# A fused transformer block in float32: where the tiles begin in a partition of the on-chip memory

## The chip, the cores and the metric

The kernel runs on one core of one Trainium2 chip. A core has five engines that run side by side: TensorE (PE in the profile; its weight loads have a row of their own, PEld), VectorE (DVE), ScalarE (ACT), GpSimd (POOL) and SyncE (SP), which here only issues DMAs. Operands lie in SBUF, an on-chip memory of 128 partitions; a tile is a range of bytes that is the same in every partition. Matmul results land in PSUM. The metric is the device time of one execution in microseconds; the span of a profile runs from the first instruction to the last.

## The reference

16 sequences of 256 tokens with 256 channels go through one block: self-attention with 16 heads of 16 channels, cross-attention to 256 context tokens, and an MLP of 1024 hidden channels.

```python
c_proj = silu(c) @ W_mod + b_mod            # six rows of 256 per sequence
x_norm = ln(x) * (1 + scale_a) + shift_a
q, k, v = split(x_norm @ W_qkv + b_qkv)
x = x + gate_a * (softmax(q k^T * scale) v @ W_proj + b_proj)
q_c = ln(x) @ W_qc + b_qc
k_c, v_c = split(ln(context) @ W_kvc + b_kvc)
x = x + softmax(q_c k_c^T * scale) v_c @ W_cproj + b_cproj
h = gelu((ln(x) * (1 + scale_m) + shift_m) @ W_mlp1 + b_mlp1)
x = x + gate_m * (h @ W_mlp2 + b_mlp2)
```

## The kernel before

**Stages.** A short start loads and splits weights. Then 32 units follow, one for each attention of each sequence (16 of self-attention, kind `s`, and 16 of cross-attention, kind `c`); work for units ahead and behind is woven into each unit. The last stage, from about 555 us, is the MLP of 16 sequences in four chunks of 256 hidden channels each.

**Precision.** A float32 factor is kept as two tiles of the matmul type float32r, a high part and the remainder: `xTh` and `xTl` for activations, `wqch` and `wqcl` and their like for weights. A product is three matmuls, high by high, high by low and low by high. Every such matmul has 256 columns of moving operand (1024 bytes of a partition) and 128 columns of weights (512 bytes), and each loads its own weights first. In the call `PE.matmul(out, weights, moving)` the second argument is the loaded one.

**The matmuls by their name in the profile** (a name is output tile, arrow, operands; the profile lists the operands by the alphabet, not by their role):

- `s` and `st` from `big`, during the units: scores and transposed scores (`s_tile`, `t_part`). Weights and moving operand are both slices of one tile `big`, which holds the stacked q and k of a unit.
- `ps_q`, `ps_k`, `ps_qc`, `ps_kc`, `ps_h`: projections with the weight matrix loaded and the activations moving (`lane`, with `tok` false). `ps_v_s`, `ps_v_c`, `ps_P_s`, `ps_P_c`: projections with the activations loaded and the matrix moving (`tok` true). Each is a lane of 12 matmuls on partitions 0 to 63 and 12 on partitions 64 to 127; `beside` issues two lanes at a time, one on each half of the partitions, so that two matmuls of 64 rows run side by side.
- `o` from `pt`, `v`: probabilities times values, four matmuls of 32 weight columns side by side (`av_part`), in plain float32.
- `psT`, `psA`, `psm`: transposes, with the identity tile `ident` moving and the data loaded.
- `ph` (`mlp_first`): first MLP product on all 128 rows; weights are slices of `wself` (which holds W_mlp1 by then), and the moving operand is `wkch`/`wkcl` or `wqch`/`wqcl`, which hold the transposed activations by then. Twelve per chunk.
- `st` or `s` from `big`, `hh`/`hl` (`mlp_second`): second MLP product on all 128 rows; weights are slices of `hh`/`hl`, and the moving operand is `big[2]`, which holds W_mlp2. Twelve per chunk.

**Order.** The lists `E_` and `PLAN` and the class `InOrder` fix the order of instructions on each engine. Line 51 is that class, through which every operation goes, so that all rows of the profile name it; groups are told apart by their tiles.

**Where tiles lie.** A pool takes a range of each partition. Pools stand behind one another in the order in which the code opens them, and within a pool tiles with their buffers stand in the order of their first use, each padded to a multiple of 32 bytes. Before the change there are two such pools, `const` and `work`, and small tiles stand between large ones.

Of the kernel before, what the change touches and what calls it, by code (L numbers as in the profile page):

```python
# [10 lines left out]
F32 = mybir.dt.float32  # L11
F32R = mybir.dt.float32r
# [4 lines left out]
P = 128  # L17
# [4 lines left out]
def pixart_block(  # L22
# [8 lines left out]
    B, N, H = x.shape  # L31
# [3 lines left out]
    NT = N // P  # L35
    KC = H // P
# [22 lines left out]

    const = ctx.enter_context(tc.tile_pool(name="const", bufs=1))  # L60
    work = ctx.enter_context(tc.tile_pool(name="work", bufs=2))
    dram = ctx.enter_context(tc.tile_pool(name="dram", bufs=2, space=bass.MemoryType.DRAM))
    psum = ctx.enter_context(tc.tile_pool(name="psum", bufs=2, space=bass.MemoryType.PSUM))

# [10 lines left out]
        return psum.tile([P, 512], F32, tag=tag, name=name, bufs=2)  # L75


    wz = const.tile([P, P], F32, name="wz")
    DVE.memset(wz, 0.0)
    ident = const.tile([P, P], F32, name="ident")  # L80
    make_identity(nc, ident)
    mhalf = const.tile([P, 2], F32, name="mhalf")
    POOL.memset(mhalf, -0.5)

    big = [const.tile([P, 2, 8, N], F32R, name=f"big{i}") for i in range(3)]
    vts = [const.tile([P, NT, NH, 32], F32, name=f"v{i}") for i in range(3)]
    mxs = [const.tile([P, 160], F32, name=f"mx{i}") for i in range(3)]
    for t_ in mxs:
        POOL.memset(t_, 0.0)
    wself = const.tile([P, 16, H], F32R, name="wself")  # L90
# [11 lines left out]
    def tok(ap, b):  # L102
        return ap[b].rearrange("(t p) h -> p t h", p=P)
# [5 lines left out]
    brow = const.tile([32, P], F32, name="brow")  # L109

    def by_parity(w):
        return w.rearrange("p k (c f) -> p k f c", f=2)

# [11 lines left out]
    def wtile(name, c):  # L125
        return [const.tile([P, KC, c], F32R, name=f"{name}{s}") for s in ("h", "l")]
# [41 lines left out]
    dummy = const.tile([P, 2], F32, name="dummy")  # L168

    def f_load():  # L170
        X[0] = work.tile([P, NT, H], F32, tag="x", name="x_0", bufs=5)
# [152 lines left out]
    def layernorm(src, name):  # L324

        o = Box()

        def stats():
            o.st = work.tile([P, NT, 6], F32, tag="bnst", name=f"st_{name}")
            for t in range(NT):  # L330
                DVE.bn_stats(o.st[:, t], src()[:, t])

        def rstd(power=True):
            o.mv = work.tile([P, NT, 2], F32, tag="bnmv", name=f"mv_{name}")
            for t in range(NT):
                DVE.bn_aggr(o.mv[:, t], o.st[:, t])
            o.rs = work.tile([P, NT], F32, tag="rstd", name=f"rs_{name}")
            if power:
                o.pow()

        def pow():
            POOL.tensor_scalar(o.rs, o.mv[:, :, 1], EPS, None, ALU.add)
            POOL.tensor_tensor(o.rs, o.rs, mhalf, ALU.pow)

        def apply(eng=E_['LN'].get(name[0])):
            o.xn = work.tile([P, NT, H], F32, tag="xn", name=f"xn_{name}", bufs=3)
            for t in range(NT):
                if eng == "act":
                    ACT.activation(o.xn[:, t], src()[:, t], AF.Identity, bias=o.nb[:, t:t + 1],
                                   scale=o.rs[:, t:t + 1])  # L350
                else:
                    (DVE if eng == "dve" else POOL).tensor_scalar(
                        o.xn[:, t], src()[:, t], o.mv[:, t, 0:1], o.rs[:, t:t + 1],
                        ALU.subtract, ALU.mult)

        def shift():
            o.nb = work.tile([P, NT], F32, tag="nb", name=f"nb_{name}")
# [249 lines left out]
    def bc_t(ap):  # L607
        return ap.unsqueeze(1).to_broadcast([P, NT, H])
# [25 lines left out]
    def build_post(u):  # L634

        b, name = u.b, f"{u.kind}{u.b}"
        W = Wp if u.kind == "s" else Wcp
        o = Box()

        def begin():  # L640
            if u.kind == "c":
                return
            G[b] = work.tile([P, 2, H], F32, tag="g", name=f"g_{b}", bufs=3)
            SP.dma_start(G[b].rearrange("p a h -> p (a h)"),
                         gd[b, 0:2].rearrange("a h -> (a h)").partition_broadcast(P))

        def gate():
            if u.kind == "c":
                return
            o.xg = work.tile([P, NT, H], F32, tag="x1", name=f"xg_{b}", bufs=7)  # L650
            POOL.tensor_tensor(o.xg, X[b], bc_t(G[b][:, 1]), ALU.add)

        def pieces(hf):
            o.ps = ps_gen(f"psA{hf}_{name}", SHORT)
            return [u.oT[hf][:, r, t * P:(t + 1) * P] for t in range(NT) for r in range(2)]

        def turn(hf):
            whole(pieces(hf), o)

        def halves(hf):  # L660
            return half_turns(pieces(hf), o)

        def norm(hf):
            if hf == 0:
                o.A = work.tile([P, NT, H], F32, tag="A", name=f"A_{name}", bufs=1)
            pv = o.ps.rearrange("p (x h c) -> p x h c", x=4, h=4)
            rc = work.tile([P, 4, 4, 1], F32, tag="rc", name=f"rc{hf}_{name}")
            DVE.reciprocal(rc, pv[:, :, :, HD:HD + 1])
            A = o.A.rearrange("p t (r f) -> p (t r) f", r=2)[:, :, 64 * hf:64 * hf + 64]
            DVE.tensor_tensor(A.rearrange("p x (h i) -> p x h i", h=4),  # L670
                              pv[:, :, :, 0:HD], rc.to_broadcast([P, 4, 4, HD]), ALU.mult)

        aT = transposed(lambda: o.A, f"a{name}", pool=True)

        def proj(half):

            if half == 0:
                o.ps = ps_gen(f"psP_{name}")
            for t in range(NT):
                for k in range(KC):  # L680
                    for a, b in (((1, 0),) if half else ((0, 0), (0, 1))):
                        PE.matmul(o.ps[:, t * H:(t + 1) * H], aT.xT[a][:, k, t * P:(t + 1) * P], W[b][:, k],
                                  start=(half == t == k == b == 0), stop=(half == 1 and t == NT - 1 and k == KC - 1),
                                  skip_group_check=True)

        def end():
            t1 = work.tile([P, NT, H], F32, tag="t1", name=f"t1_{name}")
            o.t1 = t1
            ACT.copy(t1.rearrange("p t h -> p (t h)"), o.ps)

        def add():
            t1 = o.t1
            if u.kind == "s":
                POOL.tensor_tensor(t1, t1, bc_t(G[b][:, 0]), ALU.mult)
                X1[b] = o.xg
                POOL.tensor_tensor(X1[b], o.xg, t1, ALU.add)
            else:
                POOL.tensor_tensor(t1, t1, X1[b], ALU.add)
                o.out = t1

        def store():
            if u.kind == "c":
                SP.dma_start(tok(X2d, b), o.out)

        def finish():
# [119 lines left out]
    for n, (kind, b) in enumerate(seq):  # L825
        u = Box()
# [209 lines left out]
    for n, v in (("0", u0), ("1", u1), ("2", u2)):  # L1036
        for c in "KQV":
            o = getattr(v, c)
# [58 lines left out]
    for i in range(3):  # L1097
        b = i if i < 2 else 0
        u = ahead_of_mlp(nu + i, b)
# [158 lines left out]
    last, o, q = units[-1], units[-1].post, units[-2].post  # L1258
# [97 lines left out]
```

## Time and profile before

| | us |
|---|---|
| three runs | 738.65, 738.64, 736.59 (median 738.64) |
| span of the profiled execution | 737.1 |
| PE busy | 728.8 |
| PEld busy | 643.6 |
| DVE busy | 583.4 |
| ACT busy | 556.2 |
| POOL busy | 546.9 |

The span is the profiled execution's own time as far as the profile shows it; it lies within the three runs, 1.5 below their median and 0.5 above the lowest. In the profile's rows "x128" is a count, "271/277/281" is the least, the median and the greatest duration in ns, and the ends of matmuls are modelled, so the rate at which they follow one another is read from their starts. A duration of 277 ns with a start every 115 ns means that matmuls overlap in the array's pipeline.

### The profile page before, as it was taken

How to read it: one execution, taken by the hardware profiler on the slowest of the kernel's cores; microseconds unless marked ns; L12 is line 12 of the kernel's file. 1: busy time of each engine (PE TensorE's matmuls, PEld its weight loads, DVE VectorE, ACT ScalarE, POOL GpSimd, SP SyncE). 2: the span in 40 equal slices, each digit the busy share in tenths (PEclk: the TensorE clock that was granted, in tenths of full speed). 3: DMA queues.
4: the chain of work that ended last, by engine and by line, in shares of the span. 5: the costliest groups of instructions: out<-in, count | busy, mean ns of one | idle time of the engine just before them, and what ended most of it. 6: DMA issues, size and time to landing. Idle time of an engine off the chain costs nothing.

```text
span 737.1 us, 24900 instructions
## 1 busy us (share of the span) xinstructions
PE 728.8 (99%) x10104; PEld 643.6 (87%) x10104; DVE 583.4 (79%) x1218; ACT 556.2 (75%) x961; POOL 546.9 (74%) x574
## 2 busy tenths in 40 slices
PE   9999999999999999999999999999999999999997
PEld 8888888888888888888888888888888999999997
DVE  3788898989888898988888888888745676786872
ACT  3357888888888888888888888899886665566663
POOL 6687769769696876969687898878746767767743
PEclk8899999999999999999999999999999999999999
DMA  5554243333425334342533444344211423333222
GB/s 162 203 179 145 104 174 118 122 140 119 145 96 182 117 129 148 119 145 100 178 117 138 147 156 150 118 151 148 95 60 44 116 58 101 87 100 102 83 61 57
DMA packets 67109, 90.56 MB, mean 123 GB/s; under 512 B 6194, under 2 KB 38740, under 8 KB 66996
## 3 DMA queue, kind: packets, MB, share of 16 engines
q1 hardware_dynamic: 66164, 86.88, 35.4%
q8 instruction: 80, 1.31, 0.7%
q0 software_dynamic: 560, 1.84, 0.7%
q14 instruction: 33, 0.27, 0.1%
q10 hardware_dynamic: 272, 0.26, 0.1%
HBM read 26.97 MB, written 8.46 MB: 48 GB/s over the span
## 4 chain that ended last, share of the span: by engine, by line
PE 95%; DVE 2%; POOL 1%; ACT 1%; issue 1%; POOLq 0%; ACTq 0%; DVEq 0%
PE s L51 18%; PE o L51 16%; PE st L51 16%; PE ph L51 11%; PE ps_qc L51 5%; PE ps_q L51 5%; PE ps_kc L51 4%; PE ps_k L51 3%; PE ps_v_c L51 3%; PE ps_P_s L51 3%; PE ps_v_s L51 3%; PE ps_P_c L51 2%; PE ps_h L51 1%; PE psT_q L51 1%; PE psA_c L51 1%; PE psA_s L51 1%
## 5 line engine op out<-in xcount | busy, mean ns | idle before, releaser
L51 DVE TENSOR_REDUCE mx<-s 128x2 f32<-128x512 f32 x504 | 324.5, 684 | 62.8 <-PE s L51 56.8
L51 ACT ACTIVATE pt<-st 128x1024 f32<-128x1024 f32 x252 | 259.1, 1028 | 16.6 <-PE st L51 11.0
L51 PE MATMUL s<-big 63*128 63x256 f32 (+1 forms) x1024 | 185.0, 298 | 0.5 <-DVE mx L51 0.2
L51 PEld LDWEIGHTS s<-big 63*128 63x128 f32 (+1 forms) x1024 | 132.9, 185 | 19.6 <-DVE l_kc L51 6.6
L51 PE MATMUL st<-big 64*128 64x256 f32 (+1 forms) x1024 | 134.0, 297 | 0.1
L51 POOL TENSOR_TENSOR hl<-hf,hh 128x512 fp32r<-128x512 f32 x64 | 85.5, 1340 | 54.0 <-ACT hh L51 53.6
L51 PE MATMUL o<-pt,v 128*32 128x256 f32 x2048 | 123.8, 382 | 0.0
L51 PEld LDWEIGHTS st<-big 64*128 64x128 f32 (+1 forms) x1024 | 96.2, 185 | 14.9 <-issue 12.8
L51 PEld LDWEIGHTS o<-pt,v 128*32 128x32 f32 x2048 | 60.0, 109 | 41.5
L51 ACT ACTIVATE hf<-ph,bT 128x256 f32<-128x256 f32 x114 | 47.9, 472 | 33.6 <-PE ph L51 33.6
L51 ACT ACTIVATE hh<-ph,bT 128x256 fp32r<-128x256 f32 x114 | 48.0, 473 | 25.1 <-PE s L51 13.1
L51 ACT COPY oT<-o 128x512 f32<-128x512 f32 x63 | 37.0, 587 | 32.8 <-PE o L51 32.8
L51 PE MATMUL st<-big,hh 128*128 128x256 f32 x256 | 45.3, 277 | 0.0
L51 PE MATMUL s<-big,hh 128*128 128x256 f32 x256 | 45.2, 277 | 0.0
L51 PE MATMUL ps_k<-xTh_s,wself 64*128 64x256 f32 (+1 forms) x232 | 44.8, 298 | 0.1
L51 PE MATMUL ph<-wkch,wself 128*128 128x256 f32 x224 | 44.7, 283 | 0.0
L51 PE MATMUL ph<-wqch,wself 128*128 128x256 f32 x224 | 44.6, 283 | 0.0
L51 PE MATMUL ps_q<-xTh_s,wself 64*128 64x256 f32 (+1 forms) x240 | 41.1, 287 | 0.0
L51 POOL TENSOR_SCALAR xn_c<-c,mv_c,rs_c 128x256 f32<-128x256 f32 x32 | 39.1, 1230 | 1.7
L51 PE MATMUL ps_v_s<-wself,xTh_s 64*128 64x256 f32 x224 | 38.8, 293 | 0.0
L51 PEld LDWEIGHTS st<-big,hh 128*128 128x128 f32 x256 | 38.8, 188 | 0.0
L51 PEld LDWEIGHTS s<-big,hh 128*128 128x128 f32 x256 | 38.8, 188 | 0.0
(256 smaller groups left out, 2505.2 us busy)
## 6 DMA issues: line engine op xcount, KB each, us to landing
big<-h_kc SPq DMA_DIRECT2D x32, 256.0 KB
big<-h_qc SPq DMA_DIRECT2D x32, 256.0 KB
big<-h_k SPq DMA_DIRECT2D x30, 256.0 KB
big<-h_q SPq DMA_DIRECT2D x29, 256.0 KB
g<-gd SPq DMA_DIRECT2D x16, 256.0 KB
c<-in_ctx_dram SPq DMA_DIRECT2D x16, 256.0 KB
big<-l_kc SPq DMA_DIRECT2D x16, 256.0 KB
big<-l_qc SPq DMA_DIRECT2D x16, 256.0 KB
```

What stands on the lines that cost most here:

```text
L51: i = f(*a, **k)
```

## The change

Two pools are added and two tiles are moved to the front of `const`: `brow` (512 bytes) and `bqkv` (384 bytes) now fill the space up to byte 17408, which is 17 times 1024. Then every tile in `const` and `work` has a size that is a multiple of 1024 bytes. Small constants go to the pool `edge`, and statistics and other small work tiles go to `tiny`; both lie behind `work`. No instruction is added, removed or moved on any engine, the waits and the numbers of buffers are the same, and the sizes are the same. Only start addresses differ. The table has the start of the first buffer of each tile in its partition, and what is left of it beyond a multiple of 256; the other buffers of a tile leave the same remainder unless three are given.

| tile | before | left over 256 | after | left over 256 |
|---|---|---|---|---|
| `big` | 17568 | 160 | 17408 | 0 |
| `v` | 66720 | 160 | 66560 | 0 |
| `wself` | 80928 | 32 | 78848 | 0 |
| `wqch`, `wqcl`, `wkch` to `wcpl` | 98848 | 32 | 96256 | 0 |
| `qkh` (`h_q`, `h_k`, `hh`) | 119008 | 224 | 114688 | 0 |
| `pt` | 125152 | 224 | 120832 | 0 |
| `x` | 145632 | 224 | 141312 | 0 |
| `xn`, `A`, `g`, `x1`, `xTh`, `xTl`, `qkl` (`l_q`, `l_k`, `hl`), `y` | 156128 | 224 | 151552 | 0 |
| `c`, `oT` | 216032 | 224 | 210944 | 0 |
| `t1` | 224352 | 96 | 219136 | 0 |
| `ident` | 17024 | 128 | 223744 | 0 |
| `mx` (three) | 79008 | 160, 32, 160 | 224288 | 32, 160, 32 |
| `m` | 215520 | 224 | 227808 | 224 |

Slices of these tiles that a float32r matmul reads begin at multiples of 512 bytes from the tile's start, so that they leave the tile's own remainder. Of `v` the slices begin at multiples of 128.

```diff
+    edge = ctx.enter_context(tc.tile_pool(name="edge", bufs=1))
+    tiny = ctx.enter_context(tc.tile_pool(name="tiny", bufs=2))
...
-    wz = const.tile([P, P], F32, name="wz")
+    brow = const.tile([32, P], F32, name="brow")
+    bqkv = const.tile([P, 6, B], F32, name="bqkv")
+    wz = edge.tile([P, P], F32, name="wz")
...
-    ident = const.tile([P, P], F32, name="ident")
+    ident = edge.tile([P, P], F32, name="ident")
...
-    mxs = [const.tile([P, 160], F32, name=f"mx{i}") for i in range(3)]
+    mxs = [edge.tile([P, 160], F32, name=f"mx{i}") for i in range(3)]
...
-    cpT = const.tile([P, 12, B], F32, name="cpT")
-    bqkv = const.tile([P, 6, B], F32, name="bqkv")
-    sc1 = const.tile([P, 2, 2, B], F32, name="sc1")
-    bT = const.tile([P, 40], F32, name="bT")
-    sT = const.tile([P, KC, B], F32, name="sT")
+    cpT = edge.tile([P, 12, B], F32, name="cpT")
+    sc1 = edge.tile([P, 2, 2, B], F32, name="sc1")
+    bT = edge.tile([P, 40], F32, name="bT")
+    sT = edge.tile([P, KC, B], F32, name="sT")
...
-            o.st = work.tile([P, NT, 6], F32, tag="bnst", name=f"st_{name}")
+            o.st = tiny.tile([P, NT, 6], F32, tag="bnst", name=f"st_{name}")
...
-            rc = work.tile([P, 4, 4, 1], F32, tag="rc", name=f"rc{hf}_{name}")
+            rc = tiny.tile([P, 4, 4, 1], F32, tag="rc", name=f"rc{hf}_{name}")
...
-        m = work.tile([P, P], F32R, tag="m", name=f"m_{u.n}_{hf}", bufs=1)
+        m = tiny.tile([P, P], F32R, tag="m", name=f"m_{u.n}_{hf}", bufs=1)
```

`mhalf`, `dummy`, `mv`, `rs` and `nb` move in the same way.

More of the change, by code (lines that the diff above doesn't have):

```diff
@@ L75, in ps_gen @@
         return psum.tile([P, 512], F32, tag=tag, name=name, bufs=2)
-    wz = const.tile([P, P], F32, name="wz")
+    brow = const.tile([32, P], F32, name="brow")
+    bqkv = const.tile([P, 6, B], F32, name="bqkv")
+    wz = edge.tile([P, P], F32, name="wz")
     DVE.memset(wz, 0.0)
-    ident = const.tile([P, P], F32, name="ident")
+    ident = edge.tile([P, P], F32, name="ident")
     make_identity(nc, ident)
-    mhalf = const.tile([P, 2], F32, name="mhalf")
+    mhalf = edge.tile([P, 2], F32, name="mhalf")
     POOL.memset(mhalf, -0.5)
@@ L107, in load_x @@
         SP.dma_start(X[b], tok(x, b))
-    brow = const.tile([32, P], F32, name="brow")
     def by_parity(w):
@@ L167, in pixart_block @@
     wm0, wm1, wk, wq, wv = (ts[i // 2][:, i % 2] for i in range(5))
-    dummy = const.tile([P, 2], F32, name="dummy")
+    dummy = edge.tile([P, 2], F32, name="dummy")
     def f_load():
@@ L333, in rstd @@
         def rstd(power=True):
-            o.mv = work.tile([P, NT, 2], F32, tag="bnmv", name=f"mv_{name}")
+            o.mv = tiny.tile([P, NT, 2], F32, tag="bnmv", name=f"mv_{name}")
             for t in range(NT):
                 DVE.bn_aggr(o.mv[:, t], o.st[:, t])
-            o.rs = work.tile([P, NT], F32, tag="rstd", name=f"rs_{name}")
+            o.rs = tiny.tile([P, NT], F32, tag="rstd", name=f"rs_{name}")
             if power:
@@ L356, in shift @@
         def shift():
-            o.nb = work.tile([P, NT], F32, tag="nb", name=f"nb_{name}")
+            o.nb = tiny.tile([P, NT], F32, tag="nb", name=f"nb_{name}")
             POOL.tensor_scalar(o.nb, o.mv[:, :, 0], -1.0, None, ALU.mult)
```

## The prediction

> **What bounds the kernel now.** I read the page's head and its chain first, then the busy time by stage, then PE's rows in the stages.
>
> ```profile
> span 737.1 us, 24900 instructions
> PE 728.8 (99%) x10104; PEld 643.6 (87%) x10104; DVE 583.4 (79%) x1218; ACT 556.2 (75%) x961; POOL 546.9 (74%) x574
> PE 95%; DVE 2%; POOL 1%; ACT 1%; issue 1%; POOLq 0%; ACTq 0%; DVEq 0%
> ...
> 0.00:40.00 40.00, 38.12 (x242) 33.36 (x243) 22.34 (x57) 13.05 (x31) 25.73 (x38) 0.87 0.55 182
> 40.00:555.00 515.00, 514.49 (x8359) 435.25 (x8361) 438.46 (x936) 435.81 (x677) 402.35 (x432) 1.00 0.38 133
> 555.00:590.00 35.00, 33.57 (x292) 32.77 (x285) 21.89 (x41) 22.47 (x52) 25.16 (x23) 1.00 0.30 84
> 590.00:733.00 143.00, 142.59 (x1222) 142.17 (x1221) 99.75 (x184) 84.84 (x203) 93.61 (x83) 1.00 0.30 82
> ```
>
> PE carries 95% of the chain. By stage (the first number after the comma is PE's busy time, the third from the end the granted clock) it idles 0.5 us of the 515 us of units and 0.4 us of the 143 us of MLP, both at full clock. No other engine is near its limit. So a faster DMA or a shorter wait has at most the idle time of the start and of 555 to 590 us to win, and what the change can do to the time is done through the rate at which matmuls follow each other. That rate is not one number. In the MLP both products have the same shape and the array never pauses:
>
> ```profile
> 649.33 0.39 PE L51 MATMUL st<-big,hh 128*128 128x256 f32 x2
> 649.55 0.28 PE L51 MATMUL st<-big,hl 128*128 128x256 f32 x1
> 649.67 0.39 PE L51 MATMUL st<-big,hh 128*128 128x256 f32 x2
> 649.89 0.28 PE L51 MATMUL st<-big,hl 128*128 128x256 f32 x1
> 650.01 0.39 PE L51 MATMUL st<-big,hh 128*128 128x256 f32 x2
> ...
> 650.58 0.40 PE L51 MATMUL ph<-wqch,wself 128*128 128x256 f32 x2
> 650.82 0.28 PE L51 MATMUL ph<-wqcl,wself 128*128 128x256 f32 x1
> 650.94 0.40 PE L51 MATMUL ph<-wqch,wself 128*128 128x256 f32 x2
> 651.18 0.28 PE L51 MATMUL ph<-wqcl,wself 128*128 128x256 f32 x1
> 651.30 0.40 PE L51 MATMUL ph<-wqch,wself 128*128 128x256 f32 x2
> ```
>
> Six matmuls of the second product take 650.01 - 649.33 = 0.68 us, 113.3 ns each. Six of the first take 651.30 - 650.58 = 0.72 us, 120.0 ns each. It is not chance, since every matmul of a kind agrees (least/median/greatest ns):
>
> ```profile
> L51 PE MATMUL st<-big,hh x196: 276/276/279, 589.8 to 725.7; 128*128 128x256 f32 x196
> L51 PE MATMUL ph<-wqcl,wself x100: 282/283/283, 590.6 to 727.1; 128*128 128x256 f32 x100
> ```
>
> What differs is where the operands lie. While one matmul streams its moving operand, the weights of the next are loaded, so I take the distance from the next weights' start to the moving operand's start, beyond a multiple of 256. For `ph` it is 32 - 32 = 0; for the second product 160 - 224, that is 192. The units show the same with 64 rows, two lanes side by side:
>
> ```profile
> 301.47 0.28 PE L51 MATMUL ps_qc<-xTh_q,wqch 64*128 64x256 f32 x1
> 301.48 0.28 PE L51 MATMUL ps_P_c<-wcph,xTh_ac 64*128 64x256 f32 x1
> ...
> 302.51 0.27 PE L51 MATMUL ps_qc<-xTl_q,wqch 64*128 64x256 f32 x1
> 302.55 0.28 PE L51 MATMUL ps_P_c<-wcph,xTl_ac 64*128 64x256 f32 x1
> ...
> 302.83 0.24 PE s L51 x4
> 303.07 0.24 PE st L51 x4
> ```
>
> Each lane has ten starts here, nine steps. `ps_qc` (moving 224, weights 32, distance 192) takes 1.04 / 9 = 115.6 ns a step; `ps_P_c` at the same moment, with the roles exchanged (distance 64), takes 1.07 / 9 = 118.9. The last two rows are from the chain: four score matmuls, two on each half, in 0.24 us, 120 ns a step, with both operands in `big`, distance 0. Distance 0 gives 120 in both places, 192 gives 113 to 116. I read this as two streams that hinder each other when they begin at the same place of a 256-byte round.
>
> **The change, part by part.** After it every float32r operand leaves 0, so every distance is 0, the slowest value seen.
>
> *Second MLP product, on the path.* Its distance goes from 192 to 0, its step from 113.3 to 120.0.
>
> ```profile
> L51 PE MATMUL st<-big,hh 128*128 128x256 f32 x256 | 45.3, 277 | 0.0
> L51 PE MATMUL s<-big,hh 128*128 128x256 f32 x256 | 45.2, 277 | 0.0
> L51 PE MATMUL st<-big,hl 128*128 128x256 f32 x128 | 35.4, 277 | 0.0
> L51 PE MATMUL s<-big,hl 128*128 128x256 f32 x128 | 35.4, 277 | 0.0
> ```
>
> 768 matmuls by 6.7 ns are 5.1 us. PE is the only bound there, so all of it reaches the end. ACT and POOL then wait a little longer for each chunk, which costs nothing. `ph` keeps its distance: 0.
>
> *Lanes, on the path.* Lanes that load the matrix (1584 matmuls in 40 to 555 us, 792 on each half) go from distance 192 to 0, those that load the activations (1440, 720 on each half) from 64 to 0. First and last of the grouped rows:
>
> ```profile
> L51 PE MATMUL ps_qc<-xTh_q,wqch x128: 272/277/364, 108.2 to 514.4; 64*128 64x256 f32 x128
> L51 PE MATMUL ps_P_c<-wcph,xTl_ac x112: 272/276/361, 168.9 to 544.0; 64*128 64x256 f32 x112
> ```
>
> If each lost what the steps above leave to 120, that is 792 x 4.4 + 720 x 1.1 = 4.3 us. Where a quick lane runs beside a slow one the slow one ends the piece, and only 1.1 ns is lost: 1512 x 1.1 = 1.7 us. Both pairings occur; I take 3.0.
>
> *Scores*: 2016 matmuls within `big`, distance 0 before and after: 0.
>
> *Attention values and transposes.*
>
> ```profile
> L51 PE MATMUL o<-pt,v x2044: 379/379/404, 49.6 to 555.0; 128*32 128x256 f32 x186
> L51 PE MATMUL psA_s<-ident,oT 64*128 64x64 f32 x256 | 29.3, 227 | 0.0
> ```
>
> `o` has distances of 64 and 192 by turns (slices of `v` lie 128 bytes apart) and yet least equals median, so I take 0. Its bound is 512 groups of four by 6.7 ns, 3.4 us either way. The 1296 transposes go from distance 160 to 0; two halves side by side at 3.3 ns a step bound that at 2.1 us either way, and I take 0, as a 64-column stream has little time to collide.
>
> *DMAs.* Rows of 1024 and 2048 bytes now begin at multiples of 1024. The cover is PE's own work, idle 0.5 us in the units; without that cover the gain could reach the 1.9 us that PE idles in the first 40 us, where loads are waited for. I take 0. [...]
>
> *Elementwise work* on DVE, ACT and POOL keeps its shapes, and none of these engines is the bound: 0.
>
> Sum: 5.1 + 3.0 = 8.1 us on a span of 737.1, 745.2. The span stands 1.5 below the median of the runs, which gives 746.7.
>
> **The rivals.**
>
> *Faster: the start itself counts, not the distance.* Then 32 beyond a multiple of 256 is a bad start (`ph`, 120.0), 224 a good one, and 0 may be the best. The MLP alone cannot separate this from the distance, since a cost for the moving start and one for the weights' start would fit both of its rows. If all went at the best rate seen, 113.3, `ph` would win 672 x 6.7 = 4.5 us, the lanes 792 x 2.3 + 720 x 5.6 = 5.9, the scores 1008 steps x 6.7 = 6.8: 17.2 in all, 721.5. Against it: the same tile `big`, moving, goes at 120 beside weights at 160 and at 113.3 beside weights at 224, and exchanging the roles in the lanes exchanges the rates. Where it decides: if all five groups take one common step r, the time is unchanged at r = (768 x 113.3 + 672 x 120 + 1008 x 120 + 792 x 115.6 + 720 x 118.9) / 3960 = 117.6 ns; below that the change gains.
>
> *No change: addresses are indifferent.* The two rates would come from something else that goes with the kind of matmul, say the PSUM tile or who reads it, and the time stays at 738.6. Against it: `ps_qc` and `ps_P_c` have one shape and one kind of output and differ at the same moment. [...]
>
> **How the numbers follow.** A measurement of this kernel can tell about 0.3% from no change, 2.2 us. Forecast with its mechanism 0.62: its own range goes from the lanes' and the MLP's loss half as large (742.7) to all bounds together, 5.1 + 4.3 + 3.4 + 2.1 = 14.9 (753.5). Faster rival 0.25, from 736 down to 721.5, most of it where a part of the matmuls gains. No change 0.13. A range of 728 to 753 leaves out about a third of the faster rival and a tenth of the forecast, under 2 in 10 together. Slower 0.62, same 0.13, faster 0.25.
>
> **What would show it.** Right: six matmuls of the second product in 0.72 us, their median at 283 ns as `ph`, `ph` itself unchanged, `ps_qc` at 118 ns a step or more, scores unchanged. Wrong on the mechanism: `ph` off 120 though its distance is kept. Wrong on the size: lanes that restart after each wait and never settle, so that they keep their rate. If PE's busy share fell under 98%, another engine or a DMA would have come in, which I do not expect.

## The result and the profile after

| | before | changed |
|---|---|---|
| median of nine runs each, us | 737.06 | 741.91 |
| span of the profiled execution, us | 737.1 | 740.3 |

The changed kernel is slower: ratio 1.0071, 95% interval 1.0047 to 1.0096. The forecast was 746.7, ratio 1.011, so direction and mechanism held and the size was too large.

The head of the changed kernel's page, and its busy time by stage (columns as in the prediction: PE, PEld, DVE, ACT, POOL busy with counts, then the granted clock, the DMA share and GB/s):

```profile
span 740.3 us, 24900 instructions
...
PE 733.9 (99%) x10104; PEld 649.7 (88%) x10104; DVE 587.3 (79%) x1218; ACT 556.8 (75%) x961; POOL 550.5 (74%) x574
```

```profile
0.00:40.00 40.00, 38.74 (x258) 33.67 (x259) 23.52 (x60) 13.27 (x32) 27.60 (x40) 0.91 0.55 187
40.00:555.00 515.00, 514.50 (x8348) 436.31 (x8347) 437.17 (x932) 436.40 (x678) 400.51 (x430) 1.00 0.38 132
555.00:590.00 35.00, 34.64 (x294) 34.14 (x287) 20.55 (x42) 23.22 (x54) 26.34 (x23) 1.00 0.28 84
590.00:733.00 143.00, 142.77 (x1191) 142.54 (x1190) 104.40 (x182) 83.95 (x200) 94.84 (x83) 1.00 0.29 82
```

PE is as full as before, and in the same 143 us of MLP it gets through 1191 matmuls instead of 1222. The timeline of PE at the place that the prediction showed (start and duration in us, operands, count):

```profile
649.71 0.40 PE L51 MATMUL st<-big,hh 128*128 128x256 f32 x2
649.95 0.28 PE L51 MATMUL st<-big,hl 128*128 128x256 f32 x1
650.07 0.40 PE L51 MATMUL st<-big,hh 128*128 128x256 f32 x2
650.31 0.28 PE L51 MATMUL st<-big,hl 128*128 128x256 f32 x1
650.43 0.40 PE L51 MATMUL st<-big,hh 128*128 128x256 f32 x2
...
651.27 0.28 PE L51 MATMUL ph<-wqcl,wself 128*128 128x256 f32 x1
...
651.63 0.28 PE L51 MATMUL ph<-wqcl,wself 128*128 128x256 f32 x1
...
651.99 0.28 PE L51 MATMUL ph<-wqcl,wself 128*128 128x256 f32 x1
```

Six matmuls of the second product now take 650.43 - 649.71 = 0.72 us, 120.0 ns a step instead of 113.3. The first product stays at (651.99 - 651.27) / 6 = 120.0. The grouped rows of the second product say that this is no single place: its median of 276 ns has become 283, that of `ph`.

```profile
L51 PE MATMUL st<-big,hh x250: 278/283/365, 559.8 to 728.7; 128*128 128x256 f32 x125
```

The two lanes side by side, same view, in the units:

```profile
300.37 0.28 PE L51 MATMUL ps_qc<-xTh_q,wqch 64*128 64x256 f32 x1
300.37 0.28 PE L51 MATMUL ps_P_c<-wcph,xTh_ac 64*128 64x256 f32 x1
...
301.44 0.28 PE L51 MATMUL ps_qc<-xTl_q,wqch 64*128 64x256 f32 x1
301.45 0.28 PE L51 MATMUL ps_P_c<-wcph,xTl_ac 64*128 64x256 f32 x1
```

Nine steps take 1.07 and 1.08 us, 118.9 and 120.0 ns, where they took 1.04 and 1.07.

Because the two programs run the same instructions, each matmul of one trace can be set beside its twin in the other. Four landmarks cut the span: the first `o` of unit 0, the first `o` of unit 31, the first `ph` of sequence 2 and that of sequence 15. The columns are the time up to the first landmark, the three stretches between, and the rest. The same cut is given for every kernel that follows (us, one profiled execution each).

| kernel | to unit 0 | units 0 to 31 | to `ph` of 2 | `ph` of 2 to 15 | rest | span |
|---|---|---|---|---|---|---|
| before | 49.61 | 497.48 | 22.92 | 147.54 | 19.55 | 737.1 |
| changed | 47.68 | 499.14 | 21.95 | 151.50 | 20.03 | 740.3 |
| e1_shift32 | 44.72 | 499.03 | 21.92 | 151.48 | 20.05 | 737.2 |
| e2_w2 | 47.04 | 499.15 | 21.78 | 147.55 | 19.48 | 735.0 |
| e3_lanes | 45.81 | 498.00 | 22.87 | 151.50 | 20.02 | 738.2 |
| e4_scores | 50.73 | 498.99 | 21.88 | 150.52 | 19.88 | 742.0 |
| e5_both_lanes | 44.65 | 497.55 | 22.92 | 150.83 | 20.05 | 736.0 |
| e6_ph | 47.28 | 499.05 | 21.95 | 147.63 | 19.69 | 735.6 |
| e7_ident | 46.96 | 499.20 | 21.93 | 151.48 | 20.03 | 739.6 |
| b1_lanes_w2_ph | 47.21 | 497.62 | 22.76 | 147.19 | 19.62 | 734.4 |
| b2_ph_w2 | 44.90 | 498.29 | 22.90 | 148.31 | 19.80 | 734.2 |
| b3_before_ph | 44.85 | 497.83 | 22.92 | 147.17 | 19.53 | 732.3 |
| b4_kick | 48.05 | 498.23 | 22.92 | 155.25 | 19.75 | 744.2 |

Changed against before: -1.93, +1.66, -0.97, +3.96, +0.48, together +3.2 us, the difference of the spans. The first column has another cause than the change: it goes from 44.65 to 50.73 over these kernels with the granted clock and not with their layout. The same stretch of the start in the kernel before and in e1_shift32, by the view of stages, where the granted clock is the third number from the end:

```profile
11.00:16.00 5.00, 4.38 (x20) 4.09 (x21) 1.32 (x6) 1.99 (x5) 2.19 (x3) 0.62 0.20 67
16.00:21.00 5.00, 5.00 (x26) 5.00 (x25) 2.28 (x7) 0.89 (x3) 0.80 (x1) 0.50 0.30 108
```

```profile
11.00:16.00 5.00, 5.00 (x44) 4.98 (x44) 2.23 (x10) 2.26 (x6) 2.81 (x4) 1.00 0.21 61
16.00:21.00 5.00, 4.92 (x42) 4.72 (x41) 3.88 (x12) 1.83 (x5) 1.07 (x3) 1.00 0.55 210
```

In nine of the thirteen profiles the clock falls to 0.50 for a stretch of the first 50 us, at a place that varies (12 to 22 us here, 39 to 46 in e2_w2). The longer the fall in the trace, the longer the first column: no fall in e1, e5, b2 and b3, 44.65 to 44.90; 3.4 us in e3, 45.81; 6.8 us in six kernels, 46.96 to 48.05; 10.2 us in the kernel before, 49.61; 13.7 us in e4, 50.73. What starts a fall stays open. Without the first column the change costs 1.66 - 0.97 + 3.96 + 0.48 = 5.1 us, beside 4.85 by the medians. So the comparison of kernels below goes by the stretches after the first landmark, and by the ratios, whose intervals reach 0.2 to 0.4% to either side.

The regain of 0.97 between units and MLP is a wait that became shorter. The prediction's stage of 555 to 590 us holds it. The timelines of DVE and POOL there, before the change:

```profile
562.55 2.78 DVE L51 TENSOR_SCALAR xn_m<-x,mv_m,rs_m 128x256 f32<-128x256 f32 x2 [0.33 <-POOL rs_m L51]
...
562.63 1.28 POOL L51 TENSOR_TENSOR hl<-hf,hh 128x512 fp32r<-128x512 f32 x1
563.87 1.31 POOL L51 TENSOR_TENSOR x<-x,cb 128x512 f32<-128x512 f32 x1
```

and after it:

```profile
562.30 1.71 DVE L51 TENSOR_SCALAR xn_m<-x,mv_m,rs_m 128x256 f32<-128x256 f32 x2 [0.23 <-POOL rs_m L51]
...
562.47 1.39 POOL L51 TENSOR_TENSOR hl<-hf,hh 128x512 fp32r<-128x512 f32 x1 [0.20 <-ACT hh L51]
563.83 1.33 POOL L51 TENSOR_TENSOR x<-x,cb 128x512 f32<-128x512 f32 x1
```

The two normalizations `xn_m` take 2.78 us before and 1.71 after; alone, one takes 0.40 (the median of this form in both traces). Before, the first is caught by POOL's `hl` and the second by POOL's `x`: they take 1.51 and 1.35 us, and each ends 0.15 us after that POOL operation. After, `hl` waits 0.20 us for ACT's `hh` and starts 0.17 us behind the first `xn_m` instead of 0.08, the first `xn_m` gets through ahead of it in 0.41, and only the second is caught, with 1.38. PE's transposes wait for `xn_m`, 0.49 and 0.94 us before and once 0.36 us after, and everything behind them. In all thirteen kernels above this place takes either 2.70 to 2.79 or 1.70 to 1.71 us: the long form in the seven with quicker units, where `hl` starts 0.00 to 0.08 us behind the first `xn_m`, and the short one in the six whose units take 499 us, where it starts 0.12 to 0.19 us behind. Why a DVE operation lasts longer beside one of POOL, no run here shows.

### The profile page after: what moved, and what is told of

The parts are those of the page before. It is cut to its first block, busy times and chain, and to the rows that moved or that the text cites. A ratio compares the mean times of both kernels' runs of the same rounds, so it can differ in the third digit from the quotient of the medians.

```text
span 740.3 us, 24900 instructions
## 1 busy us (share of the span) xinstructions
PE 733.9 (99%) x10104; PEld 649.7 (88%) x10104; DVE 587.3 (79%) x1218; ACT 556.8 (75%) x961; POOL 550.5 (74%) x574
## 4 chain that ended last, share of the span: by engine, by line
PE 96%; POOL 1%; DVE 1%; issue 1%; ACT 1%; POOLq 0%; ACTq 0%
PE s L51 19%; PE st L51 16%; PE o L51 16%; PE ph L51 11%; PE ps_q L51 4%; PE ps_qc L51 4%; PE ps_v_c L51 4%; PE ps_kc L51 3%; PE ps_P_s L51 3%; PE ps_k L51 3%; PE ps_v_s L51 3%; PE ps_P_c L51 2%; PE ps_h L51 1%; PE psT_q L51 1%; PE psA_s L51 1%; PE psA_c L51 1%
## 5 line engine op out<-in xcount | busy, mean ns | idle before, releaser
L51 PE MATMUL s<-big 63*128 63x256 f32 (+1 forms) x1024 | 183.1, 297 | 0.4 <-DVE mx L51 0.2
L51 POOL TENSOR_TENSOR hl<-hf,hh 128x512 fp32r<-128x512 f32 x64 | 88.7, 1390 | 53.7 <-ACT hh L51 53.7
L51 PEld LDWEIGHTS st<-big 64*128 64x128 f32 (+1 forms) x1024 | 94.6, 186 | 15.4 <-issue 12.8
L51 PE MATMUL st<-big,hh 128*128 128x256 f32 x256 | 47.4, 283 | 0.0
L51 PE MATMUL s<-big,hh 128*128 128x256 f32 x256 | 47.4, 283 | 0.0
L51 PE MATMUL ps_P_s<-wself,xTh_as 64*128 64x256 f32 x256 | 39.1, 282 | 0.0
```

The source lines that it names most:

```text
L51: i = f(*a, **k)
```

## The experiments

"Distance" is, as in the prediction, the start of the moving operand less the start of the next weights, beyond a multiple of 256 bytes. Whether the next weights count or a matmul's own was not separated: in the scan both lie at the same remainder. The first question is whether the distance, the start itself or the alignment of everything sets the time.

**m1_scan: the rate by itself.**

```python
def mm(bank, rows, m, w):      # starts of the moving operand and the weights, in bytes
    nc.tensor.matmul(ps[bank][:, :256], wt[rows, w//4:w//4 + 128], mv[rows, m//4:m//4 + 256], start=True, stop=True)
def group(rows, m, w):
    for i in range(40):
        mm(i % 2, rows, m + 1024 * (i % 2), w + 1024 * (i // 2 % 2))
```

> This kernel leaves the whole block out: it copies the first input to the output, and TensorE runs groups of 40 float32r matmuls of 256 columns with the starts of moving operand and weights moved by known numbers of bytes (A: the moving start from 0 to 240 by 16, weights at 0; B: distances 0 to 224 by 32 with the weights' start moved instead; C: both moved together; D: distances of 256 to 960; E: two lanes of 64 rows side by side). Distance theory (the step depends on the moving start less the next weights' start, modulo 256): A gives 120.0 ns a step at 0, 113.3 at 192, 117 to 119 at 64 and at 128; B gives what A gives at the same distance; C gives 120 throughout; D repeats A. Start theory (each operand's own start counts): A varies, B and C vary in ways of their own, C is not flat. Neither: all groups take the same step, and the two rates of the kernel come from something else than addresses. For E, distance theory gives 120 for 0 beside 0, and for 192 beside 64 a pace set by the slower lane, 118 to 119.

From the starts of each group's matmuls, without the first eight (ns a step, good to about 0.1; starts are counted from the beginning of the tiles `wt` and `mv`, which lie 8192 bytes apart):

| distance, A | 0 | 16 | 32 | 48 | 64 | 80 | 96 | 112 |
|---|---|---|---|---|---|---|---|---|
| step | 120.0 | 118.7 | 116.7 | 118.3 | 117.8 | 120.0 | 120.0 | 113.3 |
| **distance, A** | **128** | **144** | **160** | **176** | **192** | **208** | **224** | **240** |
| step | 118.7 | 118.7 | 117.3 | 119.1 | 113.3 | 119.1 | 118.4 | 117.1 |

C, both starts moved together: 120.0 in all seven groups. D: each distance gives the step of A at the same remainder of 256.

Lanes side by side (E): 120.0 for 0 beside 0, 113.3 for 192 beside 192. With unlike distances it depends on which half has which: both lanes take 117.8 with 192 on the lower half and 64 on the upper, but 113.3 and 117.8, each its own step, with the two exchanged. In the same way 0 below and 192 above end in 120.0 for both, and 192 below and 0 above keep 113.3 and 120.0. So the slower lane sets the pace of the other in some pairs and not in others.

The operands' addresses alone move the rate by 6%, a common start does nothing, and the round is 256 bytes at the four remainders that D tries. Two groups fall out: B at distance 192, with the moving start at 0 and the weights at 64, takes 117.8, where A, with 192 and 0, takes 113.3; and B at 160 takes 118.7, where A takes 117.3. The windows of A at 0, A at 192, B at 192, and C at 128, each 3.6 us (PE and PEld busy with counts first; the counts include the two or three matmuls that reach into a window):

```profile
22.00:25.60 3.60, 3.60 (x32) 3.60 (x31) 0.00 (x0) 0.00 (x0) 1.00 0.45 125
78.40:82.00 3.60, 3.60 (x34) 3.60 (x33) 0.00 (x0) 0.00 (x0) 1.00 0.45 141
125.80:129.40 3.60, 3.60 (x33) 3.60 (x33) 0.00 (x0) 0.00 (x0) 1.00 0.02 5
149.60:153.20 3.60, 3.60 (x32) 3.60 (x32) 0.00 (x0) 0.00 (x0) 1.00 0.00 0
```

A group also needs time to settle: A at 192 begins with steps of 116, 120, 117, 117, 123, 118 and 114 ns and only then holds 113.3.

**e1_shift32: everything 32 bytes later.**

```diff
-    mhalf = edge.tile([P, 2], F32, name="mhalf")
+    mhalf = const.tile([P, 2], F32, name="mhalf")
```

> Every large tile of the changed kernel begins 32 bytes later, so that all float32r operands leave 32, all distances stay 0, and no large tile begins at a multiple of 64 any more. Distance theory: as the changed kernel, 1.007 of the kernel before (741.9), second MLP product 120.0 a step, units as after. Alignment theory (that the tiles begin at multiples of 1024 gave something back, through transfers or elementwise work, or cost something itself): the time leaves 741.9 by over 1 us, upwards if alignment had helped (743 to 745), downwards if the aligned start itself was the cost (737). Start theory: the second product leaves 120.

740.6 us, ratio 1.0085 (1.0059 to 1.0111). The median is 1.3 us under that of the changed kernel, but the kernel before stood at 736.19 beside it, 0.9 lower than beside the changed one, and the two ratios agree within their intervals. Every stretch after the first landmark is within 0.11 us of the changed kernel. So a common start of 32 instead of 0 changes nothing that shows in this kernel's time. The first DMA queue, in the kernel before, the changed one, this one and b3_before_ph, which has the starts of the kernel before (packets, MB, share of 16 engines' span):

```profile
q1 hardware_dynamic: 66164, 86.88, 35.4%
```

```profile
q1 hardware_dynamic: 66164, 86.88, 34.6%
```

```profile
q1 hardware_dynamic: 66164, 86.88, 34.7%
```

```profile
q1 hardware_dynamic: 66164, 86.88, 35.9%
```

Of their spans that is 261, 256, 256 and 263 us; the eleven kernels with the new starts have 252 to 259. So the change did make the transfers about 2% shorter, and none of it reached the end.

**e2_w2: only W2 moved.**

```diff
...
+    const.tile([P, 48], F32, name="pad0")       # 192 bytes ahead of big[2]
     big.append(const.tile([P, 2, 8, N], F32R, name="big2"))
+    const.tile([P, 16], F32, name="pad1")
```

> The changed kernel, with only big[2] begun 192 bytes later (64 bytes of padding behind it bring the next tile back to a multiple of 256). The second MLP product gets distance 192 again, with its weights left aligned; all else keeps distance 0. Distance theory: st and s from big, hh at 113.3 a step and a median of 277, 768 x 6.7 = 5.1 us less in the MLP, 741.9 - 5.1 = 736.8, ratio to the kernel before 1.000. If the cost was the changed kernel's other edits: 741.9, ratio 1.007. If the alignment of hh and hl themselves was the cause, which stays here: 120 a step, 741.9.

737.12 us, ratio 1.0031 (1.0007 to 1.0055). The MLP's stretch returns from 151.50 to 147.55, that of the kernel before, and the units stay at 499.15. The grouped row:

```profile
L51 PE MATMUL st<-big,hh x256: 276/276/363, 558.0 to 723.7; 128*128 128x256 f32 x128
```

This is the median of before, with `hh` still aligned. The whole loss of the MLP hangs on this one distance.

**e3_lanes: only the activations moved.**

```diff
...
+                pads.append(work.tile([P, 48], F32, name="pad0", bufs=1))   # 192 bytes ahead of xTh
             hi = work.tile([P, KC, N], F32R, tag="xTh", name=f"xTh_{name}", bufs=5)
             lo = work.tile([P, KC, N], F32R, tag="xTl", name=f"xTl_{name}", bufs=5)
...
+                pads.append(work.tile([P, 16], F32, name="pad1", bufs=1))
```

> The changed kernel, with only the tiles of the activations xTh and xTl begun 192 bytes later. Lanes that load the matrix get distance 192 again, lanes that load the activations 64, as before the change; the MLP's second product keeps 0. The prediction's term for the lanes is 3.0 us (bounds 1.7 and 4.3): 741.9 - 3.0 = 738.9, ratio 1.0025. The comparison of the two traces puts 0.05 us on each unit, 1.7 in all, which is the case in which the slower lane ends each piece: 740.2, ratio 1.0043. If lanes don't care: 741.9.

740.4 us, ratio 1.0081 (1.0059 to 1.0103): by the time nothing is won. By the stretches the units win 1.14 (499.14 to 498.00) and the next stretch loses 0.92 (21.95 to 22.87), since `xn_m` is caught twice again. So the lanes do care, less than the prediction's 3.0 and less than its lower bound of 1.7, and the end does not see it.

The next four ask how far the distance carries as a rule: for operands that had it badly before the change, too.

**e4_scores: q and k in tiles of their own, 64 apart.**

```diff
-    big = [const.tile([P, 2, 8, N], F32R, name=f"big{i}") for i in range(3)]
+    bk = [const.tile([P, 8, N], F32R, name=f"bk{i}") for i in range(3)]
+    const.tile([P, 16], F32, name="pad_q")
+    bq = [const.tile([P, 8, N], F32R, name=f"bq{i}") for i in range(3)]
...
-        u.q, u.k = u.qk[:, 0], u.qk[:, 1]
+        u.q, u.k = bq[n % 3], bk[n % 3]
```

> The changed kernel, with the tile big cut into a tile for k (remainder 0) and one for q (remainder 64), everything else at 0. Scores s move k over weights q, moving start less next weights' start -64, that is 192 beyond a multiple of 256; transposed scores st move q over weights k, 64. If the distance alone sets the step: 113.3 for s, 117.8 for st, 504 x 6.7 + 504 x 2.2 = 4.5 us less in the units, 741.9 - 4.5 = 737.4. If the scan's group with the moving start at 0 and the weights at 64, which took 117.77 at the same distance of 192 as the group of 113.33, shows a pattern that counts here: 117.8 for both, 1008 x 2.2 = 2.2 us, 739.7. W2 lies in q and k of the third unit's place, so the second MLP product gets distance 64 in two of three matmuls: 768 x 2/3 x 2.2 = 1.1 us less in the MLP. If scores don't care: only that 1.1.

742.61 us, ratio 1.0075 (1.0050 to 1.0100). The units keep 498.99: a miss for both sizes, 0.15 us where 2.2 or 4.5 were expected. The MLP wins 0.98, near the 1.1 for its two matmuls of three at distance 64. From one score to the next on the same half the trace has 119.5 ns on average, against 119.8 in the changed kernel (an estimate, since the halves are told apart by the spacing of the starts). Scores come two by two on each half between lanes, and the scan needed seven steps to settle; that they are too short for it fits, but was not tested by itself.

**e5_both_lanes: a distance of 192 in both kinds of lane.**

```diff
-    wself = const.tile([P, 16, H], F32R, name="wself")
+    const.tile([P, 16], F32, name="pad_w")
+    wself = [const.tile([P, 8, H], F32R, name="wself0")]        # at 64, with wkc and wqc
...
+    const.tile([P, 32], F32, name="pad_x")
+    wself.append(const.tile([P, 8, H], F32R, name="wself1"))    # at 192, with wvc and wcp
```

> The changed kernel, with the weight matrices of the lanes that load the matrix (q and k) begun 64 bytes later and those of the lanes that move the matrix (v and the output projections) 192 bytes later, activations left at 0: distance 192 in both kinds of lane, which a common shift of the activations cannot give. If the distance alone sets the step: 113.3 in both lanes, 1512 x 6.7 = 10.1 us less in the units, 731.8. If lanes that load the matrix stay at 117.8, as the scan's group with the moving start at 0 and the weights at 64, pairs run at 115.4 to 117.8: 3.3 to 7.0 us less, 734.9 to 738.6. The MLP's first product gets distances of 0 and 128, and keeps 119 to 120. If lanes don't care, as the total time of the run with only the activations moved could be read: 741.9.

739.09 us, ratio 1.0054 (1.0018 to 1.0090). The units win 1.59 (to 497.55), a sixth of the 10.1 that the rate alone would give. By the starts in the trace, with the halves told apart in the same way, the step from one lane matmul to the next averages 116.2 ns, against 119.2 in the changed kernel, and that from score to score stays at 120: so the lanes do get quicker, by less than half of the 6.7 that the rate alone would give, and what takes the rest of the gain stays open. This is a miss, too. The MLP wins 0.67, where its first product has distance 128 in one matmul of three.

**e6_ph: only wqc and wkc moved.**

```diff
+    const.tile([P, 48], F32, name="pad0")
     Wqc = wtile("wqc", H)
-    Wkc, Wvc, Wcp = wtile("wkc", H), wtile("wvc", H), wtile("wcp", H)
+    Wkc = wtile("wkc", H)
+    const.tile([P, 16], F32, name="pad1")
+    Wvc, Wcp = wtile("wvc", H), wtile("wcp", H)
```

> The changed kernel, with only wqc and wkc begun 192 bytes later, which hold the activations in the MLP. The first MLP product, 120.0 a step before the change and after it, gets distance 192: 672 x 6.7 = 4.5 us less in the MLP by the distance theory, which says that this product could have been quicker before the change, too; the lanes of the cross-attention that load these matrices get distance 64, 120 to 117.8 at most, under 1 us. 741.9 - 4.5 = 737.4, down to 736.5. If what set the rate of this product is not addresses (its readers, its PSUM tile): 120.0, 741.9.

737.83 us, ratio 1.0023 (0.9992 to 1.0054). The MLP's stretch falls by 3.87 to 147.63, and the roles of its products are exchanged. The grouped rows, for the second product and the first (283 ns in the prediction's row of `ph`):

```profile
L51 PE MATMUL st<-big,hh x256: 274/282/365, 558.2 to 724.1; 128*128 128x256 f32 x128
...
L51 PE MATMUL ph<-wqch,wself x192: 276/276/286, 603.9 to 725.6; 128*128 128x256 f32 x192
```

So the 120.0 of `ph` in the kernel before was no property of that product.

**e7_ident: the transposes.**

```diff
+    edge.tile([P, 40], F32, name="pad0")        # 160 bytes
     ident = edge.tile([P, P], F32, name="ident")
```

> The changed kernel, with only the identity begun 160 bytes later, so that the transposes have their distance of 160 again. In the traces the units lost 1.66 us by the change; with the activations moved back they regained 1.14. If the transposes hold the rest, the units (from the first to the last unit's first attention-value matmul, 499.1 us in the changed kernel) take 498.6; if not, 499.1. Nothing else moves.

Units 499.20, one run of 741.54 us: the transposes' distance does nothing that shows. The 0.5 us between e3_lanes and the kernel before in the units (498.00 and 497.48) stays without a cause. It is not the attention values: a run of 32 `o` matmuls takes 1555 ns from first to last start in both.

**b1, b2 and b3: both products of the MLP at the good distance.** If each product alone wins 3.9 us, both should beat the kernel before.

```diff
 b1: big[2] +192; wself0 at 64, wself1, wvc and wcp at 192; wkc and wqc at 0
 b2: big[2], xTh, xTl, wkc and wqc at 192; wvc and wcp at 128; wself at 0
 b3: the kernel before, wkc and wqc 192 bytes further on (32 to 224)
```

> The changed kernel with big[2] begun 192 bytes later, the weights of the self lanes at 64 (q, k) and 192 (v, output), those of the cross lanes that move the matrix at 192, wkc and wqc left at 0. From the runs so far: second MLP product at 113.3 (3.95 us less from the first ph of sequence 2 to that of sequence 15, as in the run with W2 alone), first product with distance 192 in two of three matmuls and 64 in the third: between 2/3 of the 3.87 us that the run with wqc and wkc moved gave and all of it; units 1.2 us less than 499.1, three quarters of what both lanes moved gave. 741.9 - 4.2 - 3.3 - 1.2 = 733.2, ratio to the kernel before 0.995. If the MLP's two gains do not add (another engine becomes the bound there): 737 to 738.

> The changed kernel with big[2] and the activations xTh and xTl begun 192 bytes later, wqc and wkc at 192 and the other two cross matrices at 128; wself stays at 0. Both MLP products get distance 192 in every matmul: from the first ph of sequence 2 to that of sequence 15 the MLP takes 151.5 - 3.95 - 3.87 = 143.7 us. Units as with the activations alone moved or a little less, 498.0. 741.9 - 4.2 - 4.1 - 1.1 = 732.5, ratio to the kernel before 0.994. If the two gains don't add: 737 to 738.

> The kernel before, not the changed one, with only wqc and wkc begun 192 bytes further on (224 beyond a multiple of 256, where wself stands at 32): distance 192 for the first MLP product as for the second; the cross lanes that load these two get 0 instead of 192, at most 0.5 us. Distance theory: 147.5 - 3.9 = 143.6 us for the same stretch of the MLP, 736.9 - 4.1 + 0.4 = 733.2, ratio 0.995. If the kernel before had been at its best because of where its tiles lay by chance, or if the first product's rate has another cause: 736.9 or above.

Measured 736.57 (ratio 0.9998, 0.9973 to 1.0023), 739.06 (1.0027, 1.0003 to 1.0051) and 736.59 (0.9988, 0.9965 to 1.0011). The MLP's stretch takes 147.19, 148.31 and 147.17: the gains do not add. It is not another engine: PE is busy without a gap from 600 to 700 us in b2 and b3. In b3 the second product settles at 113.3 and the first takes 117.8, though both have distance 192:

```profile
L51 PE MATMUL st<-big,hh x256: 276/276/365, 554.4 to 720.9; 128*128 128x256 f32 x128
```

```profile
L51 PE MATMUL ph<-wqch,wself x192: 277/281/281, 601.0 to 722.4; 128*128 128x256 f32 x192
```

So the main expectations of all three kernels missed: they took each distance to have one rate. b2 shows it most plainly, as there every matmul of the MLP and every change from one product to the other has distance 192. Its stages:

```profile
585.50:594.00 8.50, 8.50 (x77) 8.50 (x76) 5.61 (x10) 6.32 (x16) 6.21 (x7) 1.00 0.34 72
598.00:640.00 42.00, 42.00 (x359) 42.00 (x358) 30.79 (x59) 25.97 (x63) 29.73 (x26) 1.00 0.29 87
640.00:720.00 80.00, 80.00 (x682) 80.00 (x681) 55.89 (x103) 47.64 (x114) 52.11 (x46) 1.00 0.31 88
```

From 574 to 594 us the starts repeat 113, 113, 114 through both products, but for four transposes at 583.1 us and six unsettled steps behind them. At 594.5 us the transposes of sequence 5 come between, with a gap of 0.82 us in PE, and from 598 us to the end the starts repeat a rhythm of nine steps of 117 to 119, mean 117.8. Same instructions, same addresses, two steady rates. B at 192 in the scan has this rhythm of nine, too.

**b4_kick: can the quick rhythm be led in?**

```diff
+        if (b, c) in ((4, 2), (6, 1)):
+            homes = homes[:1] + (("xTh", 5), ("xTl", 5))      # hh and hl at 192: distance 0
```

> The run with all MLP operands at distance 192 (both products, and both changes between them), with hh and hl of two of the 64 chunks (third chunk of sequence 4, second of sequence 6) put into buffers of xTh and xTl, which leave 192 instead of 0: the second product of these two chunks, 12 matmuls each, runs at distance 0. In that run the MLP's matmuls took 113.3 ns a step from 574 to 594 us and 117.8 from 595 us to the end, at the same distance; transposes stand between. Theory of two patterns: at distance 192 there are two steady rhythms, 113.33 and 117.77, and which one is held depends on what came before; a stretch at distance 0 (120) leads into 113.33, as where W2 alone was moved. Then after the chunk of sequence 4 all steps to the end are 113.3: from the first ph of sequence 6 to that of sequence 15, 864 matmuls, 97.9 us and some 0.2 for the second such chunk, instead of 101.8; the time 739.1 - 3.9 - 0.5 = 734.7, ratio to the kernel before 0.997 at most. If the two rates come from what other engines do at the time (their reads or writes), 117.8 returns: 101.8 and 739.1. If a stretch at distance 0 only costs its own 12 x 2.2 ns: 739.2.

745.46 us, ratio 1.0124 (1.0095 to 1.0154): a miss. After the first such chunk (608.7 to 610.1 us, twelve steps of 120) the rhythm of 117.8 was back, and the second led out of 113.3 into 117.8. But the two rhythms show again at the same operands. PE paused at the first `ph` of each of the sequences 6 to 14. After eight of these nine pauses the steps were 113.3 up to the next pause or the second such chunk, after the ninth (712.5 us) 117.8 to the end. The stages after the pause at 616 us and after the second chunk:

```profile
617.50:626.00 8.50, 8.50 (x77) 8.50 (x76) 5.93 (x11) 4.83 (x12) 6.50 (x7) 1.00 0.27 78
632.00:640.00 8.00, 8.00 (x70) 8.00 (x69) 4.75 (x10) 4.43 (x12) 4.27 (x5) 1.00 0.45 133
```

By 8.5 us that is 77 and, in proportion, 74 matmuls. The loss of time is the pauses themselves: PE idles 9.45 of the 144 us from 600 us on. That stage, and the view of waits for PE from 570 us on (what waited for what, us in all, times, the longest):

```profile
600.00:744.00 144.00, 134.55 (x1132) 131.38 (x1130) 100.75 (x171) 77.31 (x186) 85.78 (x76) 1.00 0.26 78
```

```profile
PE ph L51 <- DVE wqcl L51: 2.1, 4, 1.2
PE ph L51 <- DVE wkcl L51: 1.4, 5, 0.3
PE ph L51 <- DVE wqch L51: 1.3, 3, 0.7
PE ph L51 <- DVE wkch L51: 0.8, 2, 0.4
```

The split of the activations on DVE comes too late, in one sequence after the other. At the longest pause it was caught behind POOL, as `xn_m` was. PE, DVE and POOL at 628 us:

```profile
628.10 0.35 PE L51 MATMUL ph<-wqch,wself 128*128 128x256 f32 x1 [0.66 <-DVE wqch L51]
629.68 0.39 PE L51 MATMUL ph<-wqcl,wself 128*128 128x256 f32 x1 [1.23 <-DVE wqcl L51]
...
627.98 1.64 DVE L51 TENSOR_TENSOR wqcl<-z,wqch 128x512 fp32r<-128x512 f32 x1
...
627.76 1.31 POOL L51 TENSOR_TENSOR hl<-hf,hh 128x512 fp32r<-128x512 f32 x1 [1.17 <-ACT hh L51]
```

The subtraction into `wqcl` from `z` takes 0.69 us in all five instances of the kernel before, and 1.64 here behind `hl`. That alone does not make PE pause: in the changed kernel the same five have a median of 1.66, and PE waits for none of them. Why the split comes late in nine sequences here stays open; the quicker matmuls and the two moved chunks were not separated. The MLP's stretch grew to 155.25.

## Why the prediction was right, and where its sizes were off

**Mechanism: right for this change.** All its signs came: six matmuls of the second product in 0.72 us at a median of 283, `ph` unchanged at 120.0, `ps_qc` at 118.9, PE at 99%. The scan's group C and e1_shift32 rule out the rival in which the start itself counts. The scan and e2_w2 rule out indifference to addresses. The two starts against each other move the step of these float32r matmuls from 113.3 to 120.0 ns. That the two streams hinder each other is the reading that fits; what in the chip they share, no run here shows. What the prediction had too simple is that each distance has one rate. Distance 0 does: 120.0 wherever a run had settled. At 192 there are two, 113.3 and 117.8. The change went to 0, so this did not hurt the forecast; it broke the expectations of the b kernels.

**Second MLP product, 5.1: 4.4 measured.** 3.96 between the landmarks and 0.48 behind them. The rate was right. The term counted all 64 chunks as on the path, while five run before the first `ph` of sequence 2, where PE waits for DVE's `xn_m` anyway (1.4 us in all before the change); and it took every step of the kernel before as 113.3, while the first step within a chunk took 118.1 on average.

**Lanes, 3.0 (1.7 to 4.3): mis-sized.** The units lost 1.66, the figure of the prediction's lower case, in which the slower lane ends each piece. That it agrees so well is partly luck: in the scan the slower lane sets the pace in some pairs and not in others, and moving the activations back regains only 1.14. The rate was read at lanes with nine steps in a row. In the trace of the kernel before, 1220 of the 3024 lane matmuls from 40 to 555 us stand in such rows of 20 or more, ten on each half; the others have scores and transposes among them. That these break off before they settle is an estimate from the seven steps that the scan needed. This is the sign that the prediction named for a wrong size.

**Scores, attention values, transposes, DMAs, elementwise work, each 0:** held, but for the regain below. The units' runs of `o` take 1555 ns in both, and e7_ident shows nothing from the transposes. The transfers did get shorter: the first queue's packets take 256 us instead of 261. As the prediction had it, this was hidden: PE is as full as before. Which part of it is alignment stays open, since the packets take the same 256 us with the starts 32 bytes further on.

**Not foreseen: 1.0 us given back between units and MLP.** "ACT and POOL wait a little longer for each chunk, which costs nothing" left out that POOL starting 0.17 instead of 0.08 us behind a DVE operation lets that one pass, and that PE waits for that one.

**The base.** The sum was put on a median of 738.64 from three runs; nine runs gave 737.06. Of the 4.8 us between 746.7 and 741.91 the base holds 1.6, the lanes 1.3, the regain 1.0 and the MLP 0.7, together 4.6.

## What to carry to other kernels

Where TensorE is the bound and every matmul loads its own weights, look at where the moving operand begins against the next weights: tiles that all begin at the same remainder gave the slowest step of the scan, and a few bytes of padding between two groups of operands were worth up to 6% of a long, unbroken run there, and 2.6% of the MLP's stretch here (e2_w2 and e6_ph, 3.9 of 151.5 us). Short runs gained little of it (0.15 us in the scores of e4_scores), and a rate read at the best place of a trace is not the rate of all of them. Judge such an edit stage by stage, by the same instructions in both traces: here a stretch won back what another lost, and the start of the program varied by more than the whole effect (44.65 to 50.73 us, against 4.85).

## What the hardware showed that was not expected

- One instruction stream with one set of addresses has two steady rates: in b2_ph_w2 113.3 ns a step from 574 to 594 us, 117.8 from 598 us to the end. Changes of rhythm came at pauses, at transposes and at stretches of another distance, though not at each of them: behind the transposes at 583 us 113.3 came back. What selects the one or the other stays open: a stretch at distance 0 led into 113.3 in e2_w2 and e6_ph and into 117.8 in b4_kick, where the weights' start moved instead of the moving operand's.
- The best step in the scan, 113.3, came at distances of 112 and 192, the worst, 120.0, at 0, 80 and 96: the rate is not smooth in the distance.
- DVE operations that take 0.40 and 0.69 us alone took about 1.4 and 1.65 beside a POOL operation. For the first `xn_m` 0.04 us divides the two cases in all thirteen profiles: POOL's start up to 0.08 us behind it went with the long form, from 0.12 us on with the short one.
- The granted clock of PE fell to 0.50 for 3.4 to 13.7 us within the first 50 us of nine of the thirteen profiles, and in four it did not. In six of the nine PE had been busy throughout the 6.8 us before the fall, and in all nine it was busy throughout the fall. The span moves by up to 6 us with it (44.65 to 50.73 in the first column).

No layout was shown to beat the kernel before: the best, b3, stands at 0.9988 with an interval of 0.9965 to 1.0011. b1 and b3 are level with it: b1 undoes what the change cost, and b3 adds nothing to the kernel before.
